# Second ffn's keys of seven batches as seven block products over both token halves, with the gate in another buffer and a new written-out order

## The chip, the cores and the metric

The kernel runs on one core of a Trainium2 chip. The metric is the device time of one execution in microseconds (us); the number quoted for a kernel is the median of its runs. Engines are called by their names or by those of the profile: TensorE (PE; its weight loads are PEld), VectorE (DVE), ScalarE (ACT), GpSimd (POOL) and SyncE (SP, which only issues DMAs here).

## The reference, cut to what matters

The input x has 8 batches of 512 tokens with 256 features, all in float32. Four layers follow each other, and each adds its result to x: a linear attention (the profile's names a, kv, q, gf), an ffn (names ending in f), a softmax attention with 16 heads of 64 (n, qk, v, sc, e, cx, y) and the same ffn once more with the same weights (names ending in g). The ffn is:

```
def ffn(x, W_r, W_k, W_v, mu_r, mu_k):       # x is layer-normed
    x_prev = concatenate([zeros, x[:, :-1]]) # shifted by one token
    xr = mu_r * x + (1 - mu_r) * x_prev
    xk = mu_k * x + (1 - mu_k) * x_prev
    r = sigmoid(xr @ W_r.T)
    k = square(relu(xk @ W_k.T))             # the "keys"
    return r * (k @ W_v.T)
```

## The kernel before

**Tiling.** A batch is worked on in two halves of 256 tokens (h = 0, 1). Mixed rows lie with features on the partitions: `xr` and `xk` hold, for each half, two chunks of 128 features by 256 tokens. A product of the ffn for one half is four matmuls of 128 x 256 (two chunks in, two out) into one PSUM bank of 128 x 512.

**Buffers.** There are two sets of the buffers `xn`, `xp`, `xr`, `xk` (lines 326 to 342): "False" serves the fronts (linear attention, first ffn, norm of the attention) of batches 0 and 2 to 7 and the last batch's second ffn, "True" serves the front of batch 1 and the second ffn of batches 0 to 6. `xp` holds the transposed normed rows of the linear attention and, where rows are turned on TensorE, the shifted rows times (1 - mu_r). `ka` (the keys) lies in `xn`, and `r` (the gate) lies in `xk`.

**ffn (line 523).** For each half by itself: mix `xr` and `xk`; four matmuls k (L533); Relu from PSUM on ACT (L540), Square in place (L543); four matmuls r (L432), Tanh on ACT (L547); four matmuls o (L432); then DVE multiplies by the gate (L552) and POOL adds to x (L559). Where rows are turned by DMA (`normed_dma`, line 404), POOL splits the 16-bit halves of the float32 rows (L411), SP issues a transposing DMA (L416), and POOL puts the halves together again (L420).

**Block products.** Queries and keys of the attention (L858, names m_qk) and its values (L894, m_v) are not plain products: `seven` (line 794) computes a 2 x 2 by 2 x 2 block product in seven block matmuls instead of eight, with sums of weight blocks and of row blocks made on POOL before (L756, L775) and sums of results made by ACT and DVE after (`begin`, `join`, L814, L824, L832). Its products are issued in the order 1, 6, 7, 2, 5, 4, 3; the profile's names do not tell 2, 4, 3 from 1, 7, 5, since these share a bank.

**Attention.** Head pairs go two by two (`attend`, line 1085): 8 scores steps (L1019, 4 matmuls on quarters of the array), each followed by DVE's maximum (L1024) and two exponentials on ACT (L1035), interleaved with context steps (L1072) that need the values scaled by POOL (`vs`, L1052). I call what stands between two attention stretches a fill: it holds all the other work, and it ends with the scores of the next two pairs, which need the m_qk product of those pairs.

**Order.** All engines run in program order, and the order is fixed when the program is built: `Order` (line 77) runs generators of steps, each with an engine, an estimated cost and a time at which its input is ready, and picks by start time, due time and a triple from `CHOICES` (line 38) for each stretch. Behind a waiting instruction everything on that engine's queue waits. PSUM has 3 double banks (scores) and 2 single ones (context); fills may use all five.

Of the kernel before, what the change touches and what calls it, by code (L numbers as in the profile page):

```python
# [14 lines left out]
P = 128  # L15
# [23 lines left out]
    (-4, 2, 90203), (-4, -1, 82533), (-6, 1, 13258), (1, 2, 55349), (6, -1, 0), (6, 0, 31648),  # L39
    (6, 1, 79266), (-6, 2, 0), (6, 2, 0), (-6, 0, 0), (6, 2, 32685), (0, 0, 0), (6, -1, 57850),  # L40
    (2, 2, 0), (-2, 0, 61030), (0, 0, 8722), (0, -1, 70803), (6, -1, 0), (1, 0, 423),
    (0, 0, 1350), (-1, 0, 93496), (-6, -1, 32755), (6, 1, 0), (1, 2, 25961), (4, 0, 78747),
    (1, 2, 30264), (0, 2, 52830), (4, 2, 36824), (6, 0, 37004), (4, -1, 19765), (-2, 1, 75445),
    (0, 0, 79050), (6, 1, 84670), (4, 1, 42587),
# [32 lines left out]
class Order:  # L77
# [40 lines left out]
    def clear(self, banks):  # L118

        for i in banks:  # L120
            while not unheld(self.banks[i]):
                c = self.banks[i]
                self.run(c if c.mark in self.marks else self.first(self.able()))
# [111 lines left out]
def kernel(ctx: ExitStack, tc: tile.TileContext, a: dict, out: bass.AP):  # L235
# [92 lines left out]
    def buffers(own):  # L328


        if own not in sets:
            s = {
                n: one.tile([P, 2, 512], F32, tag=f"{n}{own}", name=f"{n}{own}")
                for n in ("xr", "xk")
            }
            for n in ("xn", "xp"):
                s[n] = one.tile([P, 2, 2, HS + 1], F32, tag=f"{n}{own}", name=f"{n}{own}")
                nc.gpsimd.memset(s[n][:, 0, :, 0:1], 0.0)

            s["ka"], s["r"] = s["xn"], s["xk"]  # L340
            sets[own] = s
        return sets[own]
# [4 lines left out]

    def inner(t, h):
        return t[:, h, :, 1:]
# [5 lines left out]
    def normed(src, name, s, h, ready, early=False):  # L355

        ready = yield "V", 1.2, ready
        mv = small.tile([P, 2, 2], F32, tag="mv", name=f"mv_{name}_{h}")
        for u in range(2):
            st = small.tile([P, 6], F32, tag="st", name=f"st_{name}_{h}_{u}")  # L360
            nc.vector.bn_stats(st, src[:, 2 * h + u, :])
            nc.vector.bn_aggr(mv[:, u, :], st)
        xn, rstd = inner(s["xn"], h), small.tile([P, 2], F32, tag="rstd", name=f"rstd_{name}_{h}")
        if early:

            ready = yield "G", 1.05, ready
            nc.gpsimd.tensor_scalar(rstd, mv[:, :, 1], LN_EPS, 1.0, ALU.add, ALU.mult)
            nc.gpsimd.tensor_tensor(rstd, rstd, neg_half[:, :2], ALU.pow)
            ready = yield "V", 0.75, ready
            for u in range(2):  # L370
                nc.vector.tensor_scalar(
                    xn[:, u, :], src[:, 2 * h + u, :], mv[:, u, 0:1], rstd[:, u : u + 1],
                    ALU.subtract, ALU.mult,
                )
        else:

            shift = small.tile([P, 2], F32, tag="shift", name=f"shift_{name}_{h}")
            ready = yield "G", 1.4, ready
            nc.gpsimd.tensor_scalar(shift, mv[:, :, 0], -1.0, None, ALU.mult)
            nc.gpsimd.tensor_scalar(rstd, mv[:, :, 1], LN_EPS, 1.0, ALU.add, ALU.mult)  # L380
            nc.gpsimd.tensor_tensor(rstd, rstd, neg_half[:, :2], ALU.pow)
            nc.gpsimd.tensor_tensor(shift, shift, rstd, ALU.mult)
            ready = yield "A", 1.0, ready
            for u in range(2):
                nc.scalar.activation(  # L385
                    xn[:, u, :], src[:, 2 * h + u, :], AF.Identity,
                    bias=shift[:, u : u + 1], scale=rstd[:, u : u + 1],
                )
        return ready

    def normed_t(src, name, s, h, ready, mark=None, early=False):

        ready = yield from normed(src, name, s, h, ready, early)
        xn = inner(s["xn"], h)
        ready = yield "T", 0.55, ready, -1, mark
        ps = bank(f"tr_{name}_{h}").rearrange("p (k s) -> p k s", k=KC)
        for kc in range(KC):
            for u in range(2):
                nc.tensor.transpose(
                    ps[:, kc, u * P : (u + 1) * P], xn[:, u, kc * P : (kc + 1) * P], ident  # L400
                )
        return ps, ready

    def normed_dma(src, name, s, h, ready, dst, mark=None):
# [3 lines left out]
        apart, turned = (s[n].bitcast(U16)[:, h, :] for n in ("xr", "xk"))  # L408
        ready = yield "G", 1.2, ready
        for u in range(2):  # L410
            nc.gpsimd.tensor_copy(  # L411
                apart.rearrange("p (l k u d) -> p l k u d", l=2, k=KC, u=2)[:, :, :, u, :],
                s["xn"].bitcast(U16)[:, h, u, 2:].rearrange("p (k d l) -> p l k d", l=2, k=KC),
# [34 lines left out]

    def mixed_t(xb, name, s, h, ready, xr, xk):
# [3 lines left out]

        parts = ((1, s["xn"]), (0, s["xp"]))
# [8 lines left out]
        for i, y in parts:  # L463
            for kc in range(KC):
                nc.scalar.activation(
                    y[:, h, kc, 1:], ps[:, kc, :], AF.Identity, scale=omu[:, i, kc : kc + 1]
                )
        order.marks[name, h] = ready
        if h == 1:
            ready = yield "V", 0.25, ready, -1, (name, 0)  # L470
            for i, y in parts:
                nc.vector.tensor_tensor(
                    y[:, 1, :, 0:1], edge[name], omu[:, i, :].unsqueeze(2), ALU.mult
                )
        for (i, y), dst in zip(parts, (xk, xr)):
            ready = yield "V", 0.79, ready
            for kc in range(KC):
                nc.vector.scalar_tensor_tensor(
                    dst[:, kc, :], ps[:, kc, :], mu[:, i, kc : kc + 1], y[:, h, kc, :HS],
# [7 lines left out]
    def mixed_dma(xb, name, s, h, ready, xr, xk):  # L487
# [4 lines left out]
            lambda: s["xr"].bitcast(U16)[:, h, :].rearrange("p (k s) -> p k s", k=KC),  # L492
# [6 lines left out]
        for i, dst in ((1, xk), (0, xr)):  # L499
# [7 lines left out]
            if h == 0:  # L507
                nc.vector.memset(ps[:, :, 0:1], 0.0)
            else:
                nc.vector.tensor_tensor(  # L510
                    ps[:, :, 0:1], edge[name], omu[:, i, :].unsqueeze(2), ALU.mult
                )
# [10 lines left out]
    def ffn(xb, name, s, h, ready, add_on, by_dma):  # L523
# [5 lines left out]
        done = yield "T", BANK, mixed  # L529
        ps = bank(f"k_{name}_{h}")  # L530
        for dc in range(KC):
            for kc in range(KC):
                nc.tensor.matmul(  # L533
                    ps[:, dc * HS : (dc + 1) * HS], lhsT=fk[:, kc, dc * P : (dc + 1) * P],
                    rhs=xk[:, kc, :], start=(kc == 0), stop=(kc == KC - 1),
                )
        done = yield "A", 0.6, done
        ka, r = inner(s["ka"], h), s["r"][:, h, :]
        ps = ps.rearrange("p (k s) -> p k s", k=KC)
        nc.scalar.activation(ka, ps, AF.Relu)  # L540
        order.give()
        squared = yield "A", 0.6, done
        nc.scalar.activation(ka, ka, AF.Square)  # L543
# [5 lines left out]
        ready = yield "T", BANK, squared  # L549
# [4 lines left out]
        return (yield from add_to(xb, h, r, ready, add_on))  # L554

# [36 lines left out]
    def linear(b, h):  # L592
# [3 lines left out]
        xt, kv = inner(s["xp"], h), inner(s["ka"], h)  # L596
# [5 lines left out]
        else:  # L602
            ready = yield from normed_dma(
                xb, f"a{b}", s, h, ready, lambda: s["xp"].bitcast(U16)[:, h, :, 2:]
# [37 lines left out]
    def queries(b, h):  # L642

        s = buffers(b == 1)
        xt = inner(s["xp"], h)
# [32 lines left out]
    def front(b, h, gf, ready):  # L678
# [10 lines left out]
        ready = yield from ffn(xb, f"f{b}", s, h, ready, adder(b), b >= 2)  # L689
# [42 lines left out]
    }  # L732

# [11 lines left out]
    def sums_of_weights(w, tag, split, after):  # L745
# [3 lines left out]
        (a11, a21), (a12, a22) = v  # L749
        s1, s2, s4 = (s[:, i, :].rearrange("p (g c) -> p g c", g=a11.shape[1]) for i in range(3))  # L750
        for dst, x0, x1, op in (
            (s1, a21, a22, ALU.add), (s2, s1, a11, ALU.subtract), (s4, a12, s2, ALU.subtract),
            (a21, a11, a21, ALU.subtract),
        ):
            ready = yield "G", 1.3, 0.0, -1, after
# [29 lines left out]
    def blocks_of_weights(w, sums, split, g):  # L785
# [5 lines left out]
        s1, s2, s4 = (sums[:, i, g * n : (g + 1) * n] for i in range(3))  # L791
        return [a11, a12, s4, a22, s1, s2, s3]

    def seven(name, sums, mul, c, begin, join):
# [5 lines left out]
        (c11, c12), (c21, c22) = c  # L800

        def product(n):
            ready = yield "T", FAST, 0.0, -1, sums
# [4 lines left out]
            return i, ps, ps.rearrange("p (u s) -> p u s", u=2), ready  # L808
# [4 lines left out]
        u2 = yield "V", 0.62, max(ready, u1)  # L813
# [4 lines left out]
        p2 = yield "T", FAST, u1, -1, None, False  # L818
        mul(b1, 2, False)
        yield from begin(ps1, c11, max(p2, u2))  # L820
        order.give(i1)
        i5, b5, ps5, p5 = yield from product(5)
        c22_done = yield "V", 0.62, max(p5, u3)
        nc.vector.tensor_tensor(c22, ps5, c22, ALU.add)  # L824
        p4 = yield "T", FAST, u3, -1, None, False
        mul(b7, 4, False)
        yield from join(ps7, c21, c12, p4, False)
        order.give(i7)
        p3 = yield "T", FAST, c22_done, -1, None, False
        mul(b5, 3, False)  # L830
        order.marks[name] = yield "V", 0.62, p3
        nc.vector.tensor_tensor(c12, ps5, c12, ALU.add)  # L832
        order.give(i5)

# [110 lines left out]
    def project_out(b, half):  # L945
# [3 lines left out]
        for tp in range(NT // 2):  # L949
# [10 lines left out]
            if half == 1:  # L960
                order.add(tail(b, tp, ready), NP * (b + 2) + 1, lead)
# [3 lines left out]
    def tail(b, h, ready):  # L965
# [7 lines left out]
        order.marks["g", b, h] = yield from ffn(x[b], f"g{b}", buffers(not last), h, ready, add_on, not last)  # L973
# [156 lines left out]
    order.add(sums_of_weights(av, "sums_v", split_values, "plain_v"), 5)  # L1130
    order.until(-1)
# [5 lines left out]
    total += 2 * FAST  # L1137
# [76 lines left out]
```

## Time and profile before

| what | us |
|---|---|
| median of 3 runs | 1154.61 (1153.1 to 1155.28) |
| the profiled execution | 1151.33 |
| its span, first to last instruction | 1149.6 |
| busy: PE, PEld | 1127.1, 702.6 |
| busy: DVE, ACT, POOL | 780.2, 671.8, 440.3 |
| first matmul starts at | 6.92 |

The profile is of one execution on the chip, and all durations come from it. A row of the groups gives the line, the engine, the operation, what it writes and reads, how many records, busy time, the mean of one in ns, and the idle time of its engine just before with what ended it. One float32 matmul of 128 x 256 leaves two PE records, so "x112" is 56 matmuls; their records overlap, and the distance from one start to the next is what a matmul takes. The granted TensorE clock is 1.000 over the whole span.

### The profile page before, as it was taken

Reading aid. Unit: us, or ns where it says so; the run is one execution under the profiler, and the core shown is the slowest. Engines: PE = TensorE matmul, PEld = TensorE weight load, DVE = VectorE, ACT = ScalarE, POOL = GpSimd, SP = SyncE. Lnnn points to the kernel's source line nnn. Section 1 sums busy time; section 2 is a strip of 40 time slices with the busy share of each in tenths; the row PEclk is TensorE's granted clock in tenths of the full one; section 3 lists DMA queues with packets and bytes.
Section 4 is the critical chain, followed back from the end, with each engine's and each line's share of the span. In section 5 each row is a group of like instructions: output and inputs, shape, how many; then the busy total and the mean of one; then the engine's idle time right before and its main releaser. Section 6 shows DMA issues by size and latency. Waiting matters only on the chain.

```text
span 1149.6 us, 19062 instructions
## 1 busy us (share of the span) xinstructions
PE 1127.1 (98%) x7020; PEld 702.6 (61%) x7020; DVE 780.2 (68%) x1403; ACT 671.8 (58%) x1763; POOL 440.3 (38%) x708
## 2 busy tenths in 40 slices
PE   7999999999999999999999899999999999999998
PEld 4645565856556676666667466567665666566557
DVE  5767658676667775867667576667676676666663
ACT  3547646475565654666544675565665367644753
POOL 4455224334324464335612436243453534312201
PEclk9999999999999999999999999999999999999999
DMA  8000001100101101011100201001010011000001
GB/s 297 1 1 2 1 1 19 20 10 11 28 1 42 24 19 28 1 46 29 37 1 1 54 12 38 11 17 40 10 29 19 19 19 25 5 10 19 11 1 37
DMA packets 61180, 28.63 MB, mean 25 GB/s; under 512 B 51456, under 2 KB 59648, under 8 KB 60576
## 3 DMA queue, kind: packets, MB, share of 16 engines
q1 hardware_dynamic: 59936, 25.70, 9.0%
q8 instruction: 56, 0.92, 0.3%
q10 hardware_dynamic: 864, 1.05, 0.3%
q0 software_dynamic: 288, 0.67, 0.2%
q14 instruction: 36, 0.29, 0.1%
HBM read 10.63 MB, written 4.19 MB: 13 GB/s over the span
## 4 chain that ended last, share of the span: by engine, by line
PE 75%; DVE 1%; DMA 0%; issue 0%; ACT 0%; POOL 0%; POOLq 0%; DVEq 0%
PE cx L1072 16%; PE sc L1019 15%; PE m_qk L858 13%; PE y L432 8%; PE m_v L894 6%; PE kv L613 3%; PE o_g L432 2%; PE r_g L432 2%; PE k_g L533 2%; PE k_f L533 2%; PE r_f L432 2%; PE o_f L432 2%; PE q L432 2%; DVE nm L1024 1%; DMA xkFalse<-xrFalse 0%
## 5 line engine op out<-in xcount | busy, mean ns | idle before, releaser
L1035 ACT ACTIVATE e<-sc,nm 128x512 f32<-128x512 f32 x512 | 347.1, 690 | 119.8 <-DVE nm L1024 119.8
L1024 DVE TENSOR_REDUCE nm<-sc 128x2 f32<-128x1024 f32 x256 | 308.9, 1218 | 76.6 <-PE sc L1019 75.7
L1072 PE MATMUL cx<-e,vs 64*64 64x512 f32 x2048 | 265.2, 590 | 5.1 <-POOL vs L1052 4.0
L1019 PE MATMUL sc<-qk 64*64 64x512 f32 x2048 | 266.8, 593 | 1.0 <-DVE qk L832 0.9
L1052 POOL TENSOR_TENSOR vs<-v,rs 128x256 f32<-128x256 f32 x128 | 78.5, 614 | 356.7 <-DVE rs L1048 348.6
L1072 PEld LDWEIGHTS cx<-e,vs 64*64 64x64 f32 x2048 | 84.3, 133 | 143.3 <-issue 117.8
L1019 PEld LDWEIGHTS sc<-qk 64*64 64x64 f32 x2048 | 75.0, 132 | 136.8 <-issue 90.7
L432 PE MATMUL y<-al,ctx 128*128 128x256 f32 x512 | 116.2, 380 | 0.0
L432 PEld LDWEIGHTS y<-al,ctx 128*128 128x128 f32 x512 | 97.0, 190 | 15.8 <-ACT e L1035 1.6
L1035 ACT ACTIVATION_READ_ACCUMULATOR e<-sc,nm 128x1 f32 x512 | 105.2, 205 | 0.0
L866 ACT ACTIVATE qk<-m_qk,bias 128x256 f32<-128x256 f32 x124 | 52.2, 476 | 56.9 <-PE m_qk L858 53.5
L1080 DVE TENSOR_TENSOR ctx<-cx,ctx 128x512 f32<-128x512 f32 x64 | 44.3, 692 | 47.6 <-ACT ctx L1079 47.6
L874 DVE SCALAR_TENSOR_TENSOR qk<-m_qk,dbias,qk 128x256 f32<-128x256 f32 x124 | 54.0, 477 | 18.3 <-PE m_qk L858 17.3
L958 DVE TENSOR_TENSOR x<-y,x 128x512 f32<-128x512 f32 x32 | 22.1, 690 | 55.3 <-PE y L432 55.3
L613 PE MATMUL kv<-wkv,xpFalse 128*128 128x512 f32 x112 | 52.2, 599 | 0.0
L1079 ACT COPY ctx<-cx 128x512 f32<-128x512 f32 x64 | 37.4, 585 | 13.8 <-PE cx L1072 13.8
L619 ACT COPY av<-kv 128x256 f32<-128x256 f32 x32 | 11.9, 373 | 54.8 <-PE kv L613 52.2
L411 POOL COPY xrFalse<-xnFalse 128x512 uint16<-128x512 uint16 x68 | 39.6, 616 | 8.5 <-ACT xnFalse L385 8.5
L559 POOL TENSOR_TENSOR x<-x,xkFalse 128x512 f32<-128x512 f32 x24 | 31.2, 1303 | 27.2 <-issue 8.7
L858 PE MATMUL m_qk<-xta,aq 128*128 128x256 f32 x124 | 39.1, 397 | 0.0
L858 PE MATMUL m_qk<-xta,sums_q 128*128 128x256 f32 x124 | 38.1, 389 | 0.7 <-DVE qk L814 0.7
L858 PE MATMUL m_qk<-xts,aq 128*128 128x256 f32 x124 | 37.2, 382 | 0.3 <-DVE qk L874 0.3
(243 smaller groups left out, 1881.6 us busy)
## 6 DMA issues: line engine op xcount, KB each, us to landing
out<-x SPq DMA_DIRECT2D x16, 256.0 KB, 2.1
x<-in_x SPq DMA_DIRECT2D x6, 512.0 KB, 4.3
aq<-in_aq SPq DMA_DIRECT2D x1, 1024.0 KB, 6.2
ak<-in_ak SPq DMA_DIRECT2D x1, 1024.0 KB, 8.1
av<-in_av SPq DMA_DIRECT2D x1, 1024.0 KB, 10.2
al<-in_al SPq DMA_DIRECT2D x1, 1024.0 KB, 12.2
xkFalse<-xrFalse SPq DMA_TRANSPOSE x34, 3.1
x<-in_x ACTq DMA_DIRECT2D x4, 128.0 KB, 4.0
```

The costliest lines, as they stand in the source:

```text
L432: nc.tensor.matmul(ps[:, u * D : (u + 1) * D], lhsT=lhs[i][:, u * P : (u + 1) * P], rhs=rhs[i], start=(i == 0), stop=(i == n - 1),)
L533: nc.tensor.matmul(ps[:, dc * HS : (dc + 1) * HS], lhsT=fk[:, kc, dc * P : (dc + 1) * P], rhs=xk[:, kc, :], start=(kc == 0), stop=(kc == K ...
L613: nc.tensor.matmul(ps, lhsT=xt[:, kc, u * P : (u + 1) * P], rhs=wkv[:, kc, :], start=(kc == 0), stop=(kc == KC - 1),)
L858: nc.tensor.matmul(ps[:, w * HS : (w + 1) * HS], lhsT=lhs[w][n - 1], rhs=block_of_rows(b, n), start=start and w == 0, stop=True, skip_grou ...
L866: nc.scalar.activation(dst[:, w, :], ps[:, w, :], AF.Identity, bias=bias[:, w, p : p + 1])
L874: nc.vector.scalar_tensor_tensor(dst[:, w, :], ps[:, w, :], dbias[:, w, p // 2 : p // 2 + 1], part[:, w, :], ALU.add, ALU.add,)
L894: nc.tensor.matmul(ps[:, u * HS : (u + 1) * HS], lhsT=block_of_rows(b, n)[:, u * P : (u + 1) * P], rhs=rhs[n - 1], start=start and u == 0, ...
L1019: nc.tensor.matmul(ps[m * HD : (m + 1) * HD, j, :], lhsT=kt[hs, keys], rhs=qt[hs, :], start=True, stop=True,)
L1024: nc.vector.tensor_reduce(nm, ps, AX.X, ALU.max, negate=True)
L1035: nc.scalar.activation(e[:, j, :], ps[:, j, :], AF.Exp, bias=nm[:, j : j + 1], accum_out=sums[g, h][:, c % 2, j : j + 1],)
L1052: nc.gpsimd.tensor_tensor(vs, vh[b, p // 4][:, 2 * h : 2 * h + 2, cols].rearrange("p t (j d) -> p t j d", j=2), rs.unsqueeze(3).to_broadca ...
L1072: nc.tensor.matmul(cx[m][j * HD : (j + 1) * HD, :], lhsT=vsc[g, c // 2][ks, c % 2, j, :], rhs=es[g, c][ks, j, :], start=(c == 0), stop=(c ...
```

## The change

The keys of the second ffn of batches 0 to 6 are computed for both halves together by `seven`: seven matmuls of 128 x 256 for a batch instead of eight. POOL makes four sums of blocks of `fk` once (`sums_f`) and four sums of blocks of `xk` for each batch (one of them in place in `xk`), ACT copies two partial results out of PSUM, DVE makes five additions of 128 x 256, and Relu and Square then run in place in SBUF for each half (`through`). Since `xk` of one half is needed until both halves' keys are done, the gate of these batches lies in `xr`. The buffer `xp` is gone: the linear attention's rows lie in `xr`, and where rows are turned on TensorE, ACT writes the shifted rows straight into `xk` and `xr` (255 columns), and DVE clears or fills the first column. `xn` loses its padding column. `clear`, which frees the banks ahead of a context, picks differently, and all of `CHOICES` is new, so that the order of all fills changes.

```diff
 CHOICES = (
-    (-4, 2, 90203), (-4, -1, 82533), (-6, 1, 13258), (1, 2, 55349), ...
+    (-4, 2, 90203), (0, 0, 0), (1, 0, 44852), (-1, 1, 50129), ...
...
-        for i in banks:
-            while not unheld(self.banks[i]):
-                c = self.banks[i]
-                self.run(c if c.mark in self.marks else self.first(self.able()))
+        while held := [c for c in (self.banks[i] for i in banks) if not unheld(c)]:
+            c = held[0]
+            if c.mark not in self.marks or (c.takes and not self.slots(self.now)):
+                able = self.able()
+                c = self.first([d for d in able if not d.takes] or able)
+            self.run(c)
...
-                for n in ("xr", "xk")
+                for n in ("xn", "xr", "xk")
-            for n in ("xn", "xp"):
-                s[n] = one.tile([P, 2, 2, HS + 1], F32, tag=f"{n}{own}", name=f"{n}{own}")
-                nc.gpsimd.memset(s[n][:, 0, :, 0:1], 0.0)
+            s["sums"] = one.tile([P, 3, HS], F32, tag=f"sums{own}", name=f"sums{own}")
...
-    def ffn(xb, name, s, h, ready, add_on, by_dma):
+    def ffn(xb, name, s, h, ready, add_on, by_dma, due):
...
+        ka, r = chunks(s["ka"], h), s["r"][:, h, :]
+        squared, mark = 0.0, None
+        if by_dma and name[0] == "g":
+            r, mark = s["xr"][:, h, :], (name, "k", h)
+            if both((name, "k")):
+                order.add(keys(name, s, mixed), *due)
+        else:
...
-        ready = yield "T", BANK, squared
+        ready = yield "T", BANK, squared, -1, mark
...
+    def keys(name, s, ready):
+        xk = [chunks(s["xk"], h) for h in range(2)]
+        (b11, b12), (b21, b22) = ([xk[h][:, kc, :] for h in range(2)] for kc in range(KC))
+        t = s["sums"]
+        yield "G", 0.0, 0.0, -1, "sums_f"
+        for dst, x0, x1 in (
+            (t[:, 1, :], b22, b12), (b12, b12, b11), (t[:, 0, :], b22, b12),
+            (t[:, 2, :], b21, t[:, 0, :]),
+        ):
+            ready = yield "G", 0.8, ready
+            nc.gpsimd.tensor_tensor(dst, x0, x1, ALU.subtract)
+        order.marks[name, "t"] = ready
+        lhs = blocks_of_weights(fk, blocks["sums_f"], split_pairs, 0)
+        rhs = [b11, b21, b22, t[:, 2, :], b12, t[:, 0, :], t[:, 1, :]]
...
+        def through(h, ready):
+            for f in (AF.Relu, AF.Square):
+                ready = yield "A", 0.6, ready
+                nc.scalar.activation(ka[h], ka[h], f)
+            order.marks[name, "k", h] = ready
+        c = [[ka[h][:, dc, :] for h in range(2)] for dc in range(KC)]
+        yield from seven(f"k_{name}", (name, "t"), mul, c, begin, join, 0.5, through)
...
-    def seven(name, sums, mul, c, begin, join):
+    def seven(name, sums, mul, c, begin, join, share=1.0, through=None):
...
+        if through:
+            order.add(through(0, max(c11_done, c21_done)), order.current.due, order.current.due - order.current.rank)
...
+    order.add(sums_of_weights(fk, "sums_f", split_pairs, None), 5)
```

On TensorE the order up to the first scores is the same in both kernels. After that every fill has other members in another sequence; the prediction names those that it speaks of. They are numbered by the scores that end them: "the fill ahead of scores 16" ends with head pairs 16 and 17, counted over all batches (8 pairs a batch).

## The prediction

> **What bounds the kernel now.** I read the page's busy times and its chain of waits first, then the waits of PE, then the groups by form, then the timeline at the longest waits.
>
> ```profile
> span 1149.6 us, 19062 instructions
> PE 1127.1 (98%) x7020; PEld 702.6 (61%) x7020; DVE 780.2 (68%) x1403; ACT 671.8 (58%) x1763; POOL 440.3 (38%) x708
> ...
> PE 75%; DVE 1%; DMA 0%; issue 0%; ACT 0%; POOL 0%; POOLq 0%; DVEq 0%
> ```
>
> The chain that ended last is PE's own queue; the other engines have a third of the span or more to spare on average. What PE lost to waits is short enough to list:
>
> ```profile
> PE tr_a L399 <- DVE xnFalse L371: 6.9, 1, 6.9
> PE cx L1072 <- POOL vs L1052: 4.0, 2, 3.4
> PE cx L1072 <- DVE v L832: 1.0, 1, 1.0
> PE sc L1019 <- DVE qk L832: 0.9, 1, 0.9
> ...
> PE m_qk L858 <- DVE qk L814: 0.7, 1, 0.7
> ...
> PE m_qk L858 <- DVE qk L874: 0.3, 1, 0.3
> ```
>
> The first row is the start. The five others lie behind 80 us and come to 6.9 us; the rows that I leave out (3.8 us) lie ahead of 63 us, where PE's order is the same in both kernels. So there are two things to gain or lose: PE's own work, and these waits.
>
> The costs, from the groups by form (mean ns is the number behind the busy time):
>
> ```profile
> L533 PE MATMUL k_g<-xkTrue,fk 128*128 128x256 f32 x112 | 26.5, 379 | 0.0
> L543 ACT ACTIVATE xnTrue<-xnTrue 128x512 f32<-128x512 f32 x16 | 10.0, 632 | 0.4
> L540 ACT ACTIVATE xnTrue<-k_g 128x512 f32<-128x512 f32 x14 | 8.4, 598 | 34.0 <-PE k_g L533 33.8
> L619 ACT COPY av<-kv 128x256 f32<-128x256 f32 x32 | 11.9, 373 | 54.8 <-PE kv L613 52.2 <-DVE xnTrue L625 2.0
> L625 DVE TENSOR_TENSOR xnFalse<-kv,av 128x256 f32<-128x256 f32 x28 | 11.8, 421 | 25.6 <-ACT sqk L621 25.6
> L775 POOL TENSOR_TENSOR xts<-xta 128x256 f32<-128x256 f32 x16 | 11.7, 733 | 1.5 <-PE m_qk L858 1.0
> L685 DVE SCALAR_TENSOR_TENSOR xkFalse<-xkFalse,rnq,gf 128x256 f32<-128x256 f32 x28 | 19.2, 741 | 3.2 <-ACT gf L673 3.2
> ```
>
> The mean of overlapping PE records is no cost. In the timeline k_g of one half starts at 625.46 and its successor at 627.18: 1.72 us for four matmuls, 0.43 each.
>
> **The seven products: -3.0 us.** A batch had 8 matmuls of keys and has 7: 7 batches x 0.43 = 3.0 us of PE's queue. A seven-product keys matmul has the shape of the old one, so the same row holds.
>
> **What the other engines get.** ACT: two copies of 128 x 256 a batch (L619, 0.37 each), and Relu now reads SBUF: no such row; it is bounded by Relu from PSUM (0.60) and Square in SBUF (0.63), I take 0.63. Together 0.8 us a batch, 5.7 in all. DVE: five additions (L625, 0.42) = 2.1 us a batch, 14.7 in all. POOL: four subtractions (L775, 0.73) = 2.9 us a batch, 20.5 in all; once four sums of 128 x 128, for which there is no row; between 128 x 2 (L380, 0.19) and 128 x 256 (0.73) I take 0.4, so 1.6 us, and these run where POOL stands 3.2 us idle until PE's qk (at 66.14). All of this lies beside PE and costs nothing by itself; where the cover fails, PE waits, and that is the third term. The dropped clears on POOL (0.1 each, at 2.8 us, ahead of POOL's 2.5 us of idling) and the 255 columns in place of 256 are worth nothing; clearing two first columns on DVE costs about 0.15 each, two at each of three places (the L472 rows take 0.15), below what I can tell.
>
> [...] I price L685 at its median of 0.48 and leave collisions to the range.
>
> **The old waits: -6.9 us.** The new order puts other instructions at all five places. The largest, 3.4 us, ends at 646.55, after the fill ahead of scores 34:
>
> ```profile
> 635.75 1.28 POOL L559 TENSOR_TENSOR x<-x,xkTrue 128x512 f32<-128x512 f32 x1
> 637.06 0.38 SPq L976 DMA_DIRECT2D out<-x  x1
> 639.27 0.38 SPq L271 DMA_DIRECT2D x<-in_x  x1
> 639.75 1.25 SPq L416 DMA_TRANSPOSE xkFalse<-xrFalse  x1
> 644.62 1.33 POOL L420 COPY xrFalse<-xkFalse 128x1024 uint16<-128x1024 uint16 x1 [5.38 <-DMA xkFalse<-xrFalse]
> 646.55 0.66 PE L1072 MATMUL cx<-e,vs 64*64 64x512 f32 x4 [3.39 <-POOL vs L1052]
> ```
>
> POOL's add ends 637.03; on SP's queue the output goes, then the load of the next x waits for that output, then the transposition waits behind the load and lands 7.6 us after the add; POOL's copy waits for it, and `vs` behind the copy. Scores 34 began at 634.2 and context needs `vs` 8.6 us later (ten steps of 0.86), so this stops PE when the add ends later than 1 us before the scores (7.6 + 1.35 copy + 0.6 vs less 8.6). In the old order o_g2 was the last product of the fill, so the add came 2.9 us after the scores began. In the new one, o_g1's last product ends 4.3 us before scores 26, o_g3's 6.0 before 42, o_g4's 8.6 before 50, and ahead of 34 the transposition is queued between the two outputs, before the load. Counting 2.2 us from the product to the end of the add (0.2, DVE 0.69, POOL 1.3), the nearest, 26, ends 2.1 us before its scores: 1.1 us in hand. Bounds: between -6.9 (none comes back) and 0 (each comes back elsewhere).
>
> **New waits: +7.5 us.** I walked the fills of the new order by the rows. The measured pattern is that of scores 6:
>
> ```profile
> 160.03 0.59 PE L858 MATMUL m_qk<-xta,sums_k 128*128 128x256 f32 x2
> 160.66 0.69 DVE L832 TENSOR_TENSOR qk<-m_qk,qk 128x512 f32<-128x512 f32 x1 [0.18 <-PE m_qk L858]
> 161.50 0.66 PE L1019 MATMUL sc<-qk 64*64 64x512 f32 x4 [0.87 <-DVE qk L832]
> ```
>
> A fill that ends with the last m_qk product makes PE wait 0.87 for DVE's addition.
> - Ahead of scores 4, 12 and 60 the new fills end so (the old order has one such): 3 x 0.87. Ahead of 60 the chain starts late behind y: 1.0. Ahead of 4 the fill is only 8.2 us of PE (the old one had 13.8), and DVE has 7.9 in it (m_qk 3.8, L685 four times 0.48, statistics 1.2, ctx 0.7, rs 0.35); half of L685 stands between the last product and the last addition: 0.87 + 0.9 = 1.8. Together 3.7.
> - Ahead of 2, kv follows its transposes without cover for ACT's copy (0.59): 0.55.
> - Ahead of 16, v, m_qk, gf and the keys share the fill: DVE 16.5 us against PE 17.3. The product m3 waits 0.2 to 1.0 for DVE, and the keys end the fill with products 2, 5, 4, 3 at 0.43 each while an addition needs 0.2 + 0.42 + 0.15: 0.9 in all.
> - Ahead of 34, o_g2_0 comes 2.15 us behind the fourth product and needs an addition, Relu and Square: 0.65. Ahead of 50, m3 waits for DVE: 0.3.
> - At the end, tr_g7_1 has o_g6_0, tr_g7_0 and o_g6_1 as cover; the old one had 1.73 us more (r_g). ACT has Relu, Square, the mixing of tr_g7_0 and the norm ahead of it: 1.2, and 0.2 for o_g6_1: 1.4.
>
> Bounds: 0, if DVE and ACT keep up as in most old fills, and 14, if each is twice as long.
>
> **Sum.** -3.0 - 6.9 + 7.5 = -2.4 us. The profiled execution took 1151.33 (span 1149.6 and 1.7 around it), so 1148.9; the median of the runs shown lies 3.3 above that execution, and I take the same difference off it: 1154.61 - 2.4 = **1152.2**.
>
> **Rivals.**
> - *The waits do not come back* (0.14). For it: the old order has fills with v, m_qk and gf together, such as ahead of scores 18, with no wait of PE. With half of my new waits the sum is -6.2: 1148.4.
> - *They eat the gain* (0.24). DVE is busy 68% on average, but single fills are full; with 2 us more of waits, in fills that I found covered, 1154.2, no change.
> - *VectorE bounds the fills with keys* (0.16), slower. Seven fills get five more additions, and L685 collides with POOL's subtractions at 1.0 each (1.498 against 0.478). If each of the seven pays one such collision, 7.0: 1159.2. It decides from DVE work within about 1 us of the fill's PE work; ahead of 16 that is so, ahead of 56 (DVE 12.5 us, PE 20.3) it is far from so, hence the low chance.
> - *PE isn't the bound, so nothing is saved* (0.04): 1154.6. The profile speaks against it: chain PE 75%. [...] The starts 0.43 us apart without gaps decide, since the shorter queue goes through at that pace.
>
> **Chances and range.** About 0.2% (2.3 us) is what a measurement of this kernel can tell from no change. The forecast has 0.42; it straddles that bound, 0.32 faster and 0.10 within. So faster 0.32 + 0.14 = 0.46, same 0.10 + 0.24 + 0.04 = 0.38, slower 0.16. The forecast's own range is 1150.0 to 1153.5. The range for 8 in 10 takes in most of the first rival and of the second and the beginning of the third, with 0.6 of its price: 1148.3 to 1156.5.
>
> **What would show it.** Right: PE's matmul records fall by 14 with k_g products of one 128 x 256 each; waits of scores for the last addition of m_qk at scores 4, 12 and 60 with 0.9 to 1.8 each; no `cx <- POOL vs` wait over 1 us; tr_g7_1 waits about 1 us for ACT. Wrong: waits of PE behind 80 us under 4 or over 11 us in all; `vs` late behind a copy again; DVE's L685 mean far over 0.74.

## The result, and the profile after

| | median | runs | profiled execution | its span |
|---|---|---|---|---|
| before | 1154.65 | 4, 1153.1 to 1155.28 | 1151.33 | 1149.6 |
| after | 1146.9 | 4, 1146.23 to 1147.02 | 1146.23 | 1144.2 |

The ratio is 0.9934 (95% interval 0.9916 to 0.9951): the changed kernel is faster by 7.75 us, where 2.4 were predicted. From one profiled execution to the other it is 5.1 us (1151.33 to 1146.23). So 2.6 us of the gain are not in this pair of traces: the kernel before was profiled 3.3 us below its median, the changed one 0.7 below its own.

From the page of the changed kernel (line numbers are here and below those of each kernel's own code):

```profile
span 1144.2 us, 19158 instructions
PE 1124.5 (98%) x7006; PEld 701.7 (61%) x7006; DVE 795.8 (70%) x1444; ACT 675.1 (59%) x1777; POOL 461.2 (40%) x736
...
PE 49%; DVE 1%; POOL 1%; issue 1%; ACT 0%; POOLq 0%; DVEq 0%
```

The reader is to see 14 PE records less, and 15.6 us more of DVE, 20.9 of POOL and 3.3 of ACT, in a span that is 5.4 us shorter. PE still holds nearly all that the chain covers (49 of 52%; before, 75 of 76%).

The waits of PE in the changed kernel (line, what PE waited for, us in all, times, longest):

```profile
PE tr_a L395 <- DVE xnFalse L367: 6.5, 1, 6.5
PE sc L1081 <- DVE qk L889: 3.0, 3, 1.3
...
PE cx L1134 <- DVE v L974: 0.6, 1, 0.6
PE tr_g L395 <- ACT xnFalse L381: 0.5, 2, 0.4
...
PE cx L1134 <- POOL vs L1114: 0.4, 1, 0.4
...
PE m_k_g L580 <- DVE xnTrue L869: 0.3, 1, 0.3
PE kv L661 <- DVE st_n L357: 0.2, 1, 0.2
PE sc L1081 <- DVE xkFalse L512: 0.2, 1, 0.2
```

Behind 80 us these are 5.2 us in all, where the kernel before had 6.9. None stands at the old five places; the 3.0 us of scores waiting for the last addition of the query and key products are new, at scores 4 (1.29), 12 (0.79) and 60 (0.88).

### The profile page after: what moved, and what is told of

It reads as the page before. It is cut to its first block, busy times and chain, and to the rows that moved or that the text cites. A ratio compares the mean times of both kernels' runs of the same rounds, so it can differ in the third digit from the quotient of the medians.

```text
span 1144.2 us, 19158 instructions
## 1 busy us (share of the span) xinstructions
PE 1124.5 (98%) x7006; PEld 701.7 (61%) x7006; DVE 795.8 (70%) x1444; ACT 675.1 (59%) x1777; POOL 461.2 (40%) x736
## 4 chain that ended last, share of the span: by engine, by line
PE 49%; DVE 1%; POOL 1%; issue 1%; ACT 0%; POOLq 0%; DVEq 0%
PE cx L1134 10%; PE sc L1081 10%; PE m_qk L917 9%; PE y L429 6%; PE m_v L953 4%; PE kv L661 2%; PE r_g L429 2%; PE o_g L429 1%; PE m_k_g L580 1%; PE r_f L429 1%; PE o_f L429 1%; PE k_f L540 1%; PE q L429 1%; DVE xkFalse L733 0%; PE k_g L540 0%
## 5 line engine op out<-in xcount | busy, mean ns | idle before, releaser
L1081 PE MATMUL sc<-qk 64*64 64x512 f32 x2048 | 263.8, 593 | 3.1 <-DVE qk L889 3.0
L1134 PE MATMUL cx<-e,vs 64*64 64x512 f32 x2048 | 262.3, 589 | 1.0 <-DVE v L974 0.6
L661 PE MATMUL kv<-wkv,xrFalse 128*128 128x512 f32 x112 | 52.5, 605 | 0.2 <-DVE st_n L357 0.2
L417 POOL COPY xrFalse<-xkFalse 128x1024 uint16<-128x1024 uint16 x22 | 29.1, 1336 | 44.1 <-DMA xkFalse<-xrFalse 44.1
```

The costliest lines, as they stand in the source:

```text
L661: nc.tensor.matmul(ps, lhsT=xt[:, kc, u * P : (u + 1) * P], rhs=wkv[:, kc, :], start=(kc == 0), stop=(kc == KC - 1),)
L1081: nc.tensor.matmul(ps[m * HD : (m + 1) * HD, j, :], lhsT=kt[hs, keys], rhs=qt[hs, :], start=True, stop=True,)
L1134: nc.tensor.matmul(cx[m][j * HD : (j + 1) * HD, :], lhsT=vsc[g, c // 2][ks, c % 2, j, :], rhs=es[g, c][ks, j, :], start=(c == 0), stop=(c ...
```

## The experiments

Each kernel is compared with the kernel before on the same chip, and several chips were used; the medians of one kernel on different chips differ by up to 1 us (the changed one: 1146.9, 1146.43 and 1145.92), so I compare on one chip where less than that matters. A ratio is always to the kernel before, with its 95% interval.

**Where the difference between the runs and the profile comes from.** First the kernel before unchanged (e1), and the same kernel with the loads of the next x of batches 4 to 7 issued behind the next transposition instead of ahead of it (e2):

```diff
+    def load_later():
+        while later:
+            _, t, rows = later.pop()
+            nc.sync.dma_start(out=t, in_=rows)
...
-        if queues is None:
+        if queues is None and b >= 4:
+            later.append((b, x[b], rows))
+        elif queues is None:
             nc.sync.dma_start(out=x[b], in_=rows)
...
             out=turned.rearrange("p (g r) -> p g r", r=P), in_=apart
         )
+        load_later()
```

> The kernel before, unchanged. Its three runs shown took 1153.1 to 1155.3, its profiled execution 1151.33 (span 1149.6): a difference of 3.3 us that the prediction carried over to the changed kernel, whose runs (1146.2 to 1147.0) turned out to lie within 0.8 us of each other. Theory A: the kernel before has a wait of PE that depends on transfers, the one of context for vs behind the transposition at 646 us (3.4 us in the first profile), and it is 3 to 6 us longer in the other executions; then this profile shows PE waits behind 80 us of 7 to 12 us that grow with the execution's time, all of the growth on that wait. Theory B: the difference lies around the span or ahead of the first matmul (6.92 us): waits behind 80 us stay at 6.9. Theory C: it lies in PE's pace all over the span: matmul starts farther apart than 0.43 us with no wait named.

Measured: 12 runs, median 1153.93, 1150.91 to 1154.72. The profiled one took 1153.0 and has the waits of the first profile (3.25 us at the same place). What is new lies behind that wait. The windows show their length, PE's busy time and record count, then the granted TensorE clock, the DMA share and GB/s:

```profile
646.00:646.25 0.25, 0.00 (x0) 1.00 0.00 0
646.25:646.50 0.25, 0.00 (x0) 0.55 0.00 0
646.75:647.00 0.25, 0.15 (x4) 0.50 0.00 0
649.25:649.50 0.25, 0.25 (x8) 0.50 0.00 0
649.50:649.75 0.25, 0.25 (x8) 0.63 0.00 0
649.75:650.00 0.25, 0.25 (x4) 1.00 0.00 0
```

PE's last matmul ends at 643.6 (641.67 + 1.93 in the next view), and at about 646.3, some 2.7 us into the idle time, the granted clock falls to 0.50; it comes back at 649.7, 3.4 us later. PE starts again at 646.85 and so works 2.8 us at half speed. The pace shows it: in the timeline, eight records of context take 1.76 us from start to start (646.85 to 648.61), not the 0.86 at a clock of 1.00 (636.94 to 637.80 in the first profile).

```profile
641.67 1.93 PE L1019 MATMUL sc<-qk 64*64 64x512 f32 x16
646.85 1.98 PE L1072 MATMUL cx<-e,vs 64*64 64x512 f32 x8 [3.25 <-POOL vs L1052]
648.61 1.57 PE L1019 MATMUL sc<-qk 64*64 64x512 f32 x8
650.01 1.03 PE L1072 MATMUL cx<-e,vs 64*64 64x512 f32 x8
```

In the first profile of before the clock stayed at 1.00 there (windows 643.16:646.55, without a matmul, and 646.55:650.00): that execution was one without the drop. Position by position (the start of the same matmul in both traces), e1's trace loses 1.3 us against it right behind this wait and 0.2 or less anywhere else behind 11 us. The 29 runs of before on this chip (12 and 17) fall in two groups: three at 1150.5 to 1150.9, 26 at 1153.0 to 1154.8. None of the theories A, B, C had it right: the wait is the same in each profile, and the growth lies in PE's pace, but in one place, behind that wait.

> The kernel before with one thing moved: the load of the next x of batches 4 to 7 is issued on SP's queue behind the next transposition instead of ahead of it; the instructions of PE, DVE, ACT and POOL and their order are the same. If the wait of 3.4 us at 646 us is the load's doing, as the prediction reads it, cx <- vs falls from 4.0 to about 0.6 and the span from 1149.6 to about 1146.2; by theory A above, runs fall by 3 to 7 us and come closer together (within 1 us). Rival: the transposition itself is late, and the time stays within 1 us of the kernel before.

Measured: 1146.93, five runs from 1146.72 to 1147.81; ratio 0.9946 (0.9935 to 0.9958), that is -6.7 us. Both waits of context for `vs` (4.0 us) are gone from its list, and every run has a mean clock of 1.0. The trace shows the mechanism that the prediction read:

```profile
637.59 1.27 SPq L426 DMA_TRANSPOSE xkFalse<-xrFalse  x1
...
639.55 0.38 SPq L271 DMA_DIRECT2D x<-in_x  x1
...
640.81 1.35 POOL L431 COPY xrFalse<-xkFalse 128x1024 uint16<-128x1024 uint16 x1 [1.53 <-DMA xkFalse<-xrFalse]
...
642.08 0.61 POOL L1063 TENSOR_TENSOR vs<-v,rs 128x256 f32<-128x256 f32 x1
```

The transposition is issued at 637.59, ahead of the load, and not at 639.75 behind it; POOL's copy runs at 640.81 instead of 644.62, and `vs` is ready in time. So loads moved past transpositions took away 4.0 us of waits and, as the difference to 6.7, 2.7 us more: nearly as much as the whole change, with eight products and the old order. I put the 2.7 down to the half clock, which was there before in most runs and is in none of these. The runs of e1 support it: the three shorter ones (median 1150.75) lie 3.8 us above e2, about the 4.0 of the waits, and the other 26 (median 1153.85) 3.1 above those three. The trace of e1 shows only some 1.4 of it (2.8 us at half speed); 12 of the 29 runs had a lower mean clock than that execution (0.996 against 0.999), so more time at half, but no trace was taken of one, and the size of the rest is argued from the runs alone.

**What an order is worth.** The kernel before with the changed kernel's `CHOICES` and `clear`:

> The kernel before (eight matmuls for the keys, two more buffers) with the changed kernel's numbers for the planner and its clear function, so that it gets a third order of its own. It asks what an order is worth with the work of before. Theory: PE's work is that of before, 1127.1 busy, and only the waits differ; the old order had 6.9 us behind 80 us and the new 5.2, and a third one I expect between 4 and 14: 1148 to 1158, with the time following the waits to within 1 us. Rival: the numbers for the planner carry the gain by themselves: as fast as the changed kernel plus the seven products, 1150 or less.

Measured: 1242.66, ratio 1.0779 (1.0763 to 1.0794), 89 us slower: both theories miss by far. Behind the first matmul its waits come to 78 us in 39 places (10.7 in 13 in the kernel before), among them:

```profile
PE sc L1021 <- ACT e L1037: 17.3, 4, 13.3
PE cx L1074 <- POOL vs L1054: 14.6, 4, 7.6
PE cx L1074 <- DVE xrTrue L516: 12.1, 3, 5.4
```

PE's busy time is 1150.0, 22.9 more than with the same matmuls before, at a mean clock of 0.982: the half clock again. Here the triples of `CHOICES` carry no gain of their own: with other steps than those that they were chosen for they make a far worse order. The waits of this third order could not be guessed from those of the other two.

**The seven products alone.** One of them issued twice in each of the seven batches:

```diff
-            nc.tensor.matmul(
+            for _ in range(2 if n == 1 else 1):
+                nc.tensor.matmul(
```

> The changed kernel, in which the first of the seven products of the keys is computed twice in each of the seven batches (the second overwrites the first), so that a batch has eight matmuls of 128 x 256 again; every other engine's instructions and the order of all are the same. Theory: PE is the bound, so +7 x 0.43 = +3.0 us against the changed kernel, 1149.9 by its median of 1146.9, some tenths less where PE waits behind such a product anyway. Rival (PE's matmul time isn't the bound): no change, 1146.9.

Measured: 1149.03 (1148.04 to 1149.85), ratio 0.9962 (0.9951 to 0.9974); against 1146.9 on another chip +2.1. Since chips differ by as much as the open part, it was repeated beside the changed kernel:

> The changed kernel once more, for the three that follow to be compared with on the same chip: 1146.2 to 1147.0.

> The eighth product put back, as before, now beside the changed kernel. Theory: +3.0 us less the parts that fall into waits of PE that are there anyway, +2.3 to +3.0. Rival: as much as half of it is hidden, +1.5.

Measured: 1145.92 and 1149.03, +3.1 (ratios to before 0.9934, 0.9922 to 0.9947, and 0.9963, 0.9950 to 0.9975). The two medians differ by 1 us, so the traces decide: position by position, e14 falls behind e13 in seven steps of about 0.44 us, 3.1 in all, as the prediction took, and gains back 0.5 at two places (at one of them, 623 us, a key product's wait of 0.3 is gone). That leaves 2.6 us behind the first 11 us, and the same 2.6 from the first trace of the changed kernel to e3; 1.5 of the 4.1 us between the two profiled executions lie at the start.

**A wait of a chosen length.** If a wait of some 3 us makes the clock drop, it can be made on purpose. The first try added idle work on POOL ahead of one `vs`, three additions in one run (e7) and five in the next (e8, shown), beside the changed kernel itself (e5):

```diff
+        if (g, h) == (40, 0):
+            for _ in range(5):
+                nc.gpsimd.tensor_tensor(idle, idle, idle, ALU.add)
         vs = vsc[g, h] = halves_v.tile([P, 2, 2, HD], F32, tag="vs", name=f"vs_{g}_{h}")
```

> The changed kernel, unchanged, on the chip of the three that follow, for them to be compared with. Its runs took 1146.2 to 1147.0; the same is expected, 1146.9, and a granted clock of 1.0 in every run, since its longest wait of PE behind the start is 1.3 us.

> The changed kernel with a wait of PE made on purpose at one place: POOL adds an idle tile to itself three times (128 x 512, 1.28 us each) just ahead of vs of scores 40, first half; 3.8 us less the cover of about 1.4 us that vs has there make a wait of about 2.4 us. Theory (the kernel before lost its wait of 3.4 us and on top of it 1.5 to 4 us in which the granted clock was half: 0.50 from 646.4 to 649.6 us in its second profile, and 26 of 29 runs at 1153.0 to 1154.8 against three at 1150.5 to 1150.9): a wait of 2.4 us is too short for the clock to drop, so +2.4, 1149.3, clock 1.0. Rival (any wait of some us drops it): +4 to +6 us and a clock under 1.0.

> The same with five additions of the idle tile, 6.4 us less 1.4, a wait of about 5.0 us. Theory: the clock drops behind it in every run, so +5.0 and 1.5 to 3.5 us more, 1153.4 to 1155.4, with a granted clock of 0.50 for some 3 us or more behind the wait. Rival (the clock's drop in the kernel before had nothing to do with its wait): +5.0, 1151.9, and no stretch below 1.0.

Measured: 1146.43 (ratio 0.9941, 0.9928 to 0.9953), 1146.18 (0.9939, 0.9926 to 0.9951), 1146.18 (0.9937, 0.9924 to 0.9949): no wait at all, a miss of the experiment. The additions ran at 725.3 to 730.8, and `vs` was not due before 739.8, when DVE's reciprocal was there: POOL had 14.5 us of idle time. Work that must be late has to wait for the same thing, so next the scaling itself was repeated, seven, eleven (shown) and five times more:

```diff
-        nc.gpsimd.tensor_tensor(
+        for _ in range(12 if (g, h) == (40, 0) else 1):
+            nc.gpsimd.tensor_tensor(
```

> The wait on purpose again, with work that cannot run ahead: the idle additions of the last two runs started while POOL stood idle (14.5 us ahead of this vs) and were over before the scaling was due. Now vs of scores 40, first half, is written seven times more (0.6 us each, 4.2 us); it ends 740.4 in the changed kernel's profile and context takes it at about 742.4, so 2.0 of it is covered and PE waits about 2.3 us. Theory: too short for the clock to drop, +2.3 on 1146.4 to 1146.9, about 1148.9, clock 1.0 in the wait's neighbourhood. Rival (any wait of some us drops it): +4 to +6 and a stretch at 0.50.

> The same with eleven more, 6.6 us less 2.0, a wait of about 4.7 us. Theory: the clock drops behind it in most or all runs, so +4.7 and 1.5 to 3.5 more, 1152.8 to 1155; runs without the drop, if any, at about 1151.4. Rival (the drop in the kernel before had nothing to do with its wait): all runs at about 1151.4 with the clock at 1.0.

> The wait on purpose with five more scalings in place of seven: from 2.7 us measured with seven, less 2 x 0.65, about 1.4 us. Theory: no drop of the clock at 1.4 us: +1.4, all runs within 1 us of 1148.0. Rival (a drop in part of the runs at any wait over 1 us): runs in two groups 2 us apart.

| scalings more | wait in the profile | median, ratio to before | runs |
|---|---|---|---|
| 5 | 1.4 | 1148.26, 0.9954 (0.9940 to 0.9968) | 1147.28 to 1148.78, no gap of 2 us between them |
| 7 | 2.7 | 1149.73, 0.9963 (0.9948 to 0.9978) | 1148.47, 1148.79, 1148.88 at a mean clock of 1.0; 1150.58, 1150.73, 1151.80 at 0.998 |
| 11 | 5.5 | 1154.71, 1.0003 (0.9992 to 1.0013) | 12 runs, 1152.51 to 1155.47, all at 0.997 to 0.998 |

With 5 more the profiled execution took 1147.52 and the clock stays at 1.00 behind the wait. Its median is 2.3 above the changed kernel on the same chip (1145.92), where 1.4 was forecast; from trace to trace it is 1.8, the 1.4 of the wait and 0.4 at the start, and the rest has no row. With 5.5 us every run drops, by its mean clock. The windows of the profiled one:

```profile
745.50:746.00 0.50, 0.00 (x0) 0.95 0.00 0
746.00:746.50 0.50, 0.00 (x0) 0.50 0.00 0
752.00:752.50 0.50, 0.50 (x8) 0.50 0.00 0
752.50:753.00 0.50, 0.50 (x8) 0.72 0.00 0
```

The clock is half from 745.95 to 752.8, 6.8 us, twice the stretch of the kernel before. PE restarts at 748.74 and loses (752.8 - 748.74) / 2 = 2.0 us on top of the 5.5. With 2.7 us, by the mean clocks of the runs (the profiled one has no drop), half of them drop, and they are 1.7 to 3.3 us slower than those that do not; my theory had no drop there. The rival (the drop had nothing to do with the wait) falls with the longest wait.

The length of a wait alone does not decide whether the clock drops. At 646 us of the kernel before, 3.39 us left it at 1.00 in the first profile and 3.25 us halved it in e1. The trace of e4, which has many waits, has both in one execution: one of 2.47 us leaves the clock at 1.00 and one of 2.42 us halves it:

```profile
400.57 1.09 PE L1074 MATMUL cx<-e,vs 64*64 64x512 f32 x8 [2.47 <-DVE xkTrue L516]
901.28 1.98 PE L1074 MATMUL cx<-e,vs 64*64 64x512 f32 x8 [2.42 <-DVE xrTrue L516]
```

```profile
398.00:401.00 3.00, 0.53 (x8) 1.00 0.00 0
901.00:901.25 0.25, 0.00 (x0) 0.76 1.14 208
904.50:904.75 0.25, 0.25 (x8) 0.92 0.00 0
```

Worked out from the windows shown, the clock falls at 901.13 here, 2.3 us behind the start of the wait (901.28 - 2.42 = 898.86), and is back at 904.54, 3.4 us later. In e1 and e10 it falls 2.7 us behind the start (646.27 against 643.60, and 745.95 against 743.24). In the first profile of the changed kernel it falls at the end, at 1143.94 (window 1143.90:1144.20 at 0.57), 4.3 us behind the end of PE's last matmul at 1139.60. What decides whether and when it falls was not shown: these are readings of traces, with matmul ends that the profile models, and no run was made to tell the causes apart.

A shorter wait in the kernel before, with half of each load ahead of the transposition (the diff is against the kernel of e2):

```diff
-            later.append((b, x[b], rows))
+            nc.sync.dma_start(out=x[b][:, 0:2, :], in_=rows[:, 0:2, :])
+            later.append((b, x[b][:, 2:4, :], rows[:, 2:4, :]))
```

> The kernel before with half of each next x (256 KB) loaded ahead of the transposition and half behind it; nothing else moves. The transposition still waits on SP's queue for the output to land (1.7 us later than with the whole load behind it) but shares the transfer engines with half as much. The wait of context for vs should lie between 1.3 and 3.4 us, about 2.2. Theory (the wait costs itself, and the clock drops only if it comes near 3.3 us): 1146.9 + 2.2 = 1149.1, clock 1.0 in nearly all runs, runs close together. Rival (the drop comes with any such wait): 1151 to 1153 with the clock at 0.996 to 0.999.

Measured: 1151.58 (12 runs, 1150.24 to 1153.12), ratio 0.9976 (0.9967 to 0.9985). The wait is 2.0 us, as expected, and in the profiled run (1150.31) the clock stays at 1.00 behind it. But ten of the other runs are up to 2.8 us longer at a mean clock of 0.997 or 0.998, and the median lies in the rival's range, not at the 1149.1 of my theory. That looks like the drop; no trace of such a run was taken, and the mean clock also counts the end of the span, where PE is done (the 0.57 above). Whether 2.0 us is enough, or the wait was longer in those runs, stays open.

**The cover of the other engines.** POOL's subtractions and DVE's additions doubled in part:

```diff
-            nc.gpsimd.tensor_tensor(dst, x0, x1, ALU.subtract)
+            for _ in range(1 if dst is b12 else 2):
+                nc.gpsimd.tensor_tensor(dst, x0, x1, ALU.subtract)
```

```diff
-            nc.vector.tensor_tensor(dst, ps, part, ALU.add)
+            for _ in range(2):
+                nc.vector.tensor_tensor(dst, ps, part, ALU.add)
...
-        nc.vector.tensor_tensor(c12, ps6, c11, ALU.add)
+        for _ in range(2 if through else 1):
+            nc.vector.tensor_tensor(c12, ps6, c11, ALU.add)
```

> The changed kernel, in which POOL does three of the four new subtractions of 128 x 256 in each of the seven batches twice: 21 more at 0.73 us, 15.3 us of POOL; no other engine's instructions change. The prediction held POOL's work for covered: then the time stays within 1 us of the changed kernel. Rival (its collisions with VectorE's scaling by gf, median 0.478 and up to 1.498 us in the kernel before, reach PE): +4 to +15 us, and that group's mean goes up.

> The changed kernel, in which VectorE does three of the five new additions of 128 x 256 in each of the seven batches twice: 21 more at 0.42 us, 8.8 us of VectorE in the fills with keys; the other engines' instructions are the same. The prediction held VectorE's additions for covered, then +0 to +1. Doubling POOL's subtractions cost +2.7 in three new waits, so I expect some waits here as well, of key products and of scores for the additions: +1 to +3. The prediction's slower rival (VectorE bounds the fills with keys): +6 or more.

Measured: 1149.09 with POOL's (ratio to before 0.9964, 0.9950 to 0.9977; +2.7 against 1146.43 on the same chip) and 1148.51 with DVE's (0.9950, 0.9937 to 0.9964; +1.6 to +2.6 against the medians of the changed kernel on other chips, as I had expected by then). With POOL's work doubled the list has

```profile
PE cx L1135 <- POOL vs L1115: 1.9, 2, 1.2
PE m_qk L918 <- DVE qk L880: 1.1, 1, 1.1
```

1.5 us more on `vs` and 1.1 on an addition, 2.6 of the 2.7; the scaling by gf goes from a mean of 0.704 to 0.746 us. With DVE's the products of the keys wait 1.5 us where it was 0.3; this and the other changes of its list explain 0.8 us, the rest has no row. Both forecasts of the prediction, no cost and a bound on VectorE, are off: the cover holds nearly all of the change's own work, with little to spare.

**An attempt at a better version.** The last addition of a pair of heads in two, the queries' half first:

```diff
-        nc.vector.tensor_tensor(c12, ps5, c12, ALU.add)
+        for w in (range(2) if name[:2] == "qk" else (slice(None),)):
+            nc.vector.tensor_tensor(c12[:, w], ps5[:, w], c12[:, w], ALU.add)
```

> The changed kernel, in which the last addition of a pair of heads (128 x 512, 0.69 us) is made in two, first the queries' half, then the keys' (128 x 256, about 0.42 each); the first scores need of it the queries' half alone. Nothing else changes. Theory (the three waits at scores 4, 12 and 60 are lost time of PE): each falls by about 0.27, from 3.0 in all to about 2.2, and the time by 0.8, to about 1145.8; it would be the fastest kernel of the study. Rival (the 31 further instructions on VectorE, 0.15 each, cost as much elsewhere): no change or some tenths more.

Measured: 1145.45 (1144.91 to 1146.79) beside 1145.92 of the changed kernel; ratios to before 0.9933 (0.9920 to 0.9945) and 0.9934 (0.9922 to 0.9947). The three waits fell as forecast, from 3.0 to

```profile
PE sc L1082 <- DVE qk L890: 1.1, 2, 0.6
PE sc L1082 <- ACT xnFalse L381: 1.0, 1, 1.0
```

but the 0.5 us cannot be told from no change, and two of its runs lie above 1146.5.

## Why the prediction was wrong

The direction was right, the size was not. Its steps, with what the runs showed:

| step | predicted | found |
|---|---|---|
| seven products | -3.0 | -3.1 (seven steps in the trace of e14) |
| old waits gone | -6.9 | -6.9, and -2.7, put down to the half clock behind the longest (e2: -6.7 for 4.0 of waits) |
| new waits | +7.5 | +5.2 (profile) |
| ahead of 80 us | 0 | -0.7 |
| sum | -2.4 | -8.2; measured -7.75 |

**The step that failed** is the last of the sum: "the median of the runs shown lies 3.3 above that execution, and I take the same difference off it". The prediction took those 3.3 us for a constant that the changed kernel keeps; its own difference is 0.7, and the other 2.6 belonged to the kernel before, whose three runs shown were all 1.8 to 4.0 us slower than the profiled execution. This was a cost that most runs had and the trace did not. With it, the wait at 646.55 was worth about 6 us and not the 3.4 that its row shows. The changed kernel lacks this cost: its longest wait behind the start is 1.3 us, and the mean clock was 1.0 in all of its 14 runs (the first ones, e5 and e13). The second miss, nearly as large, is the term of new waits: 7.5 was summed and 5.2 came.

The signs that the prediction had named for being right came true, or nearly so, but for the last: 14 records less, waits at scores 4, 12 and 60 of 0.8 to 1.3 us, no late `vs`, and 0.5 us in two waits at the end in place of about 1. All of them are read from one profiled execution, so none could show the step that failed.

**New waits.** The places and the order of sizes were right for scores: 1.29, 0.79 and 0.88 against 1.8, 0.87 and 1.0. At scores 4 the timeline of the changed kernel shows DVE's scaling by gf between the last product and the last addition, as expected:

```profile
132.96 0.59 PE L917 MATMUL m_qk<-xta,sums_k 128*128 128x256 f32 x2
133.22 0.88 DVE L733 SCALAR_TENSOR_TENSOR xkFalse<-xkFalse,rnq,gf 128x256 f32<-128x256 f32 x2
...
134.02 0.68 DVE L889 TENSOR_TENSOR qk<-m_qk,qk 128x512 f32<-128x512 f32 x1
...
134.85 1.09 PE L1081 MATMUL sc<-qk 64*64 64x512 f32 x8 [1.29 <-DVE qk L889]
```

Too large were the fills ahead of 16 (0.9, found none), 50 (0.3, none) and 2 (0.55, found 0.2) and the end (1.4, found 0.5). Ahead of 34 the forecast 0.65 for the second half's o came as 0.3 of a key product and 0.6 of context for v, other waits than named. I had added up latencies as if nothing else stood between; which of them was too long in each fill was not taken apart.

**Old waits** went as walked: ahead of scores 34 the transposition (635.01) is now issued ahead of the load (639.24). Elsewhere it still stands behind a load (771.29 behind 770.75), but PE does not wait there. `vs` keeps PE waiting once, 0.4 us at scores 30, a place that I had not listed.

**Ahead of 80 us** I left 3.8 us of waits out because PE's order is the same there. One of them, `v <- DVE v` with 0.7, is gone all the same: POOL's order had changed. This is read from the timelines and was not tried. In the timeline of the kernel before, two normalisations of DVE meet POOL's 128 x 512 sum of aq and take 2.62 us:

```profile
57.79 2.62 DVE L371 TENSOR_SCALAR xnTrue<-x,mv_f,rstd_f 128x256 f32<-128x256 f32 x2
...
58.95 1.31 POOL L756 TENSOR_TENSOR sums_q<-aq 128x512 f32<-128x512 f32 x1
```

In the changed one the small sums of fk stand first on POOL, and the same two take 1.81:

```profile
57.79 1.81 DVE L367 TENSOR_SCALAR xnTrue<-x,mv_f,rstd_f 128x256 f32<-128x256 f32 x2
...
58.95 0.50 POOL L806 TENSOR_TENSOR sums_f<-fk 128x128 f32<-128x128 f32 x1
```

**The other engines' work** has the prices taken from the rows of before (groups by form of the changed kernel):

```profile
L733 DVE SCALAR_TENSOR_TENSOR xkFalse<-xkFalse,rnq,gf 128x256 f32<-128x256 f32 x28 | 18.4, 704 | 4.4 <-ACT gf L721 4.4
...
L598 ACT ACTIVATE xnTrue<-xnTrue 128x512 f32<-128x512 f32 x28 | 17.4, 633 | 12.3 <-DVE xnTrue L592 9.5 <-DVE xnTrue L889 2.1
...
L573 POOL TENSOR_TENSOR sumsTrue<-xkTrue 128x256 f32<-128x256 f32 x14 | 10.2, 728 | 6.6 <-DVE xkTrue L512 6.2
```

Relu and Square from SBUF take 0.633, the subtractions 0.73, as taken. The scaling by gf has a mean of 0.704 (before 0.741), so with the 28 new subtractions on POOL it took no longer than before. One place shows a meeting: two scalings beside an addition to x and a subtraction on POOL take 2.04 us (313.44), where the median of one is 0.478. The prediction's 1.498 stood beside POOL's addition of 128 x 512 at 627.27 of the first profile.

**Rivals.** "The waits do not come back" (1148.4) came nearest in time, but only 2.3 of the 3.8 us that set it apart from the forecast were fewer waits; the 2.7 us of the clock stood in no rival. "They eat the gain" and "VectorE bounds the fills" fell with 5.2 us of waits. "PE isn't the bound" fell with e14.

## What to carry to other kernels

When all runs shown are slower than the profiled execution, the trace lacks something that the runs have: look for a wait of TensorE of some us (2.42 us in e4 was followed by half clock), and count with it the half clock that can follow, which cost some 1.4 to 3 us here and came behind the same wait in some runs and not in others. Before an order is searched or products are saved, look at what stands in front of a late transfer on its queue: moving loads behind transpositions gave 6.7 us without touching the instructions of TensorE, VectorE, ScalarE or GpSimd. A term of waits that was walked by hand is better given by its bounds than by its sum, since the other engines' order also changes where the bounding engine's does not.

## What the runs showed of the hardware that I had not expected

- The granted clock of TensorE fell to 0.50 while PE waited and stayed there after its matmuls had started again: for 3.4 us in e1 (646.3 to 649.7) and e4 (901.13 to 904.54), for 6.8 in e10 (745.95 to 752.8). Eight records of context took 1.76 us in that time in e1, not 0.86.
- The same program has runs with and without the drop (1150.5 to 1150.9 and 1153.0 to 1154.8). By the runs' times and mean clocks, a wait of 2.7 us dropped it in three of six runs (e9), 3.3 us in 26 of 29 (the kernel before), 5.5 us in 12 of 12 (e10); in the trace of e4 one of 2.42 us did and one of 2.47 us did not.
- Two normalisations of 128 x 256 on VectorE took 2.62 us beside a sum of 128 x 512 on GpSimd and 1.81 beside sums of 128 x 128.
